# The query product of a window attention block, from quarters of TensorE's array to halves

## The chip, the cores and the metric

The kernel runs on one core of a Trainium2 chip. The metric is the device time of one execution in microseconds (us); lower is better. Five engines matter here: PE is TensorE (matrix products), PEld the loads of its stationary operand, which run beside it, DVE is VectorE, ACT is ScalarE, POOL is GpSimd. SP issues most DMAs.

## The reference

The input x has 32 sequences of 512 tokens with 256 features. One transformer block is computed in float32. In `[...]` are shapes.

```python
x = x + attn(layernorm(x))       # x [32, 512, 256]
x = x + ffn(layernorm(x))

# attn: 16 heads of 64, 4 key/value heads, causal window of 128
q = rmsnorm((x @ wq.T).reshape(B, T, 16, 64), q_norm_w)   # the query product: 256 -> 1024
k = rmsnorm((x @ wk.T).reshape(B, T, 4, 64), k_norm_w)
v = (x @ wv.T).reshape(B, T, 4, 64)
scores = where(0 <= i - j < 128, q . k / 8, -inf)
y = softmax(scores) @ v
return y @ wo.T

# ffn: a product of 256 x 256, and 8 gated low-rank pairs of rank 16
gate = softmax(x @ gate_w.T)
return x @ weight.T + (gate-weighted sum of V_e (U_e x)) / 16
```

The change touches only how the query product `x @ wq.T` is put on TensorE.

## The kernel before

**Tiles.** The work is cut into 128 tiles of 128 tokens (4 for each sequence). A tile passes through a pipeline of some 17 steps: layer norm statistics, the turned input xT (features on partitions, `trx`), the key/value product `kv_pe` (line 447), the query product (`qa_pe` and `qb_pe`, lines 486 and 491), norms of q and k, the scores in four parts `s_pe(3)` to `s_pe(0)` (line 606), softmax, the weighted values `y_pe` and `yb_pe` (lines 722 and 739), the output product `o_pe` (line 757), and the second half with `ug_pe`, `base_pe` and `lora_pe` (lines 813, 816, 863; the product's own line is 808 for the first two, 864 for the third).

**Order.** Nothing is scheduled by the compiler. The order on every engine is the order in which the program calls these steps. For the tiles in the middle that order is in `slot(i)` (line 894), called for i from 17 to 127; the pipeline is filled by a list of steps by hand, FIRST, and drained by another, LAST. On TensorE a slot calls, each for another tile:

`s_pe(0)`, `kv_pe`, `ug_pe`, `base_pe`, `o_pe`, `lora_pe`, `s_pe(3)`, `y_pe`, `s_pe(2)`, `qa_pe`, `yb_pe`, `s_pe(1)`, `qb_pe`, and then `s_pe(0)` of the next slot.

In each slot the steps `kv_pe` to `lora_pe` use the whole array of 128 rows by 128 columns, and everything from `s_pe(3)` to the next `s_pe(0)` uses quarters of 64 rows by 64 columns. So the array changes from quarters to the whole and back once in a slot. Over the whole program the order holds 157 changes from quarters to the whole and 157 back.

**The query product.** Its result for a tile is 128 tokens by 1024 columns and fills two PSUM banks, `q0` and `q1`, of 512 columns each; the 256 input features come in two chunks `c` of 128 partitions. The first six tiles use `q_pe` (line 463) on the whole array. The other 122 use `q_product` (line 473), called twice. `qa_pe` is the pass with r = 0: the upper 64 partitions of each chunk go to bank `q0`, the lower 64 to bank `q1`. `qb_pe` is the pass with r = 1, with the banks swapped, and so completes both sums. In a pass, for each chunk, each half m of the 128 tokens (64 columns of the stationary operand xT, written to 64 partitions of the bank) and each bank, there is one matmul that streams 512 columns of `wq_sb`. That is 8 matmuls of the program. Each float32 matmul of the program appears as two pairs of a weight load and a matmul in the profile, so a pass has 16 records, and the 122 tiles have 122 x 2 x 16 = 3904.

After `qa_pe`, ACT reads one column of bank `q1` (`q_mark`, line 499). After `qb_pe`, ACT reads both banks twice: `q_copy` (line 502, records at line 505) and `qsq` (line 507, records at line 510).

Of the kernel before, what the change touches and what calls it, by code (L numbers as in the profile page):

```python
# [19 lines left out]
ND = D // P  # L20
# [11 lines left out]
def tile_window_attn_lora_ffn(  # L32
# [45 lines left out]
    nc = tc.nc  # L78
# [8 lines left out]
    H = P // 2  # L87
# [194 lines left out]
    wq_sb = const.tile([P, ND, QD], F32, name="wq_sb")  # L282
# [11 lines left out]
    for c in range(NB):  # L294
        rows = slice(c * BL, (c + 1) * BL)
# [12 lines left out]
    for e, cmp in enumerate((ALU.is_ge, ALU.is_gt)):  # L308
        rows = slice(e * H, (e + 1) * H)
# [106 lines left out]
    class Tile:  # L416
# [55 lines left out]

        def q_product(self, r, start, stop):
            for c in range(ND):
                for m in range(2):
                    for gp in (r, 1 - r):
                        rows = slice((gp ^ r) * H, (gp ^ r) * H + H)
                        nc.tensor.matmul(  # L478
                            self.ps[f"q{gp}"][m * H : (m + 1) * H, :],
                            self.xT[rows, c, m * H : (m + 1) * H],  # L480
                            wq_sb[rows, c, gp * 512 : (gp + 1) * 512],
                            start=(start and c == 0), stop=(stop and c == ND - 1),
                            skip_group_check=True,
                        )

        def qa_pe(self):
            for gp in range(GP):
# [694 lines left out]
```

## Time and profile before

| what | value |
|---|---|
| median of 3 runs | 1947.53 us (1945.81 to 1948.91) |
| profiled execution, its own time | 1946.66 us |
| its span, first to last instruction | 1944.9 us |
| granted TensorE clock, mean | 1.000 |
| matmuls of the query product, line 478 | 3904, mean 590 ns, 64 x 64 of the array, 512 columns |
| its weight loads | 3904, mean 133 ns, 64 columns |
| matmuls of kv, line 450 | 512, mean 618 ns, 128 x 128 of the array, 512 columns |
| its weight loads | 512, mean 189 ns, 128 columns |
| PE busy from 300 to 1700 us | 1400.0 of 1400 us |

How to read it: the profile's lines give the program's line, the engine, the operation, output and inputs, the part of the array (rows\*columns), the shape, a count, the busy time and the mean duration. Matmuls are pipelined: the duration of one runs from its start to its modelled end and overlaps the next, so the time that a stage holds TensorE is read from the starts of stages, or from the chain of work that ended last, in which each piece is counted once.

### The profile page before, as it was taken

How to read it: one execution, taken by the hardware profiler on the slowest of the kernel's cores; microseconds unless marked ns; L12 is line 12 of the kernel's file. 1: busy time of each engine (PE TensorE's matmuls, PEld its weight loads, DVE VectorE, ACT ScalarE, POOL GpSimd, SP SyncE). 2: the span in 40 equal slices, each digit the busy share in tenths (PEclk: the TensorE clock that was granted, in tenths of full speed). 3: DMA queues.
4: the chain of work that ended last, by engine and by line, in shares of the span. 5: the costliest groups of instructions: out<-in, count | busy, mean ns of one | idle time of the engine just before them, and what ended most of it. 6: DMA issues, size and time to landing. Idle time of an engine off the chain costs nothing.

```text
span 1944.9 us, 61511 instructions
## 1 busy us (share of the span) xinstructions
PE 1931.6 (99%) x21677; PEld 1332.0 (68%) x21677; DVE 1714.8 (88%) x4958; ACT 1523.6 (78%) x6407; POOL 1628.1 (84%) x1103
## 2 busy tenths in 40 slices
PE   8999999999999999999999999999999999999999
PEld 4566676676677666766766777667667666776677
DVE  6999889998989988899889899888998898998894
ACT  6888777877888787778878777887787787877783
POOL 6998889888898888898888988888988889888872
PEclk9999999999999999999999999999999999999999
DMA  5676767767676676776676767776776767667663
GB/s 128 140 157 156 157 154 158 156 154 159 156 158 155 155 160 155 156 160 153 155 158 155 160 154 158 158 157 152 157 159 154 159 154 161 152 153 161 145 145 93
DMA packets 273060, 297.90 MB, mean 153 GB/s; under 512 B 172272, under 2 KB 206704, under 8 KB 272752
## 3 DMA queue, kind: packets, MB, share of 16 engines
q1 hardware_dynamic: 272208, 292.40, 67.3%
q8 instruction: 172, 2.82, 0.7%
q10 hardware_dynamic: 544, 1.57, 0.2%
q14 instruction: 136, 1.11, 0.2%
HBM read 36.71 MB, written 16.78 MB: 28 GB/s over the span
## 4 chain that ended last, share of the span: by engine, by line
PE 91%; SPq 5%; ACT 1%; DVE 1%; DMA 1%; issue 1%; POOL 1%; ACTq 0%; DVEq 0%; POOLq 0%
PE o_ps L760 21%; PE q_ps L478 20%; PE y_ps L709 15%; PE s_ps_S L620 12%; PE kv_ps L450 11%; PE f_ps L808 5%; SPq L401 4%; PE g_ps L808 3%; PE f_ps L864 3%; ACT ex L648 1%; DMA pT<-tr 1%; SPq L269 1%; PE q_ps L466 1%; DVE tr L414 0%; POOL other L688 0%
## 5 line engine op out<-in xcount | busy, mean ns | idle before, releaser
L648 ACT ACTIVATE ex<-s_ps_S,nmax 128x128 f32<-128x128 f32 x2048 | 719.6, 373 | 17.3 <-DVE nmax L637 10.4
L660 POOL TENSOR_TENSOR ex<-ex,rden 128x1024 f32<-128x1024 f32 x256 | 485.3, 1896 | 238.4 <-DVE rden L656 238.3
L478 PE MATMUL q_ps<-wq_sb,xT 64*64 64x512 f32 x3904 | 470.8, 590 | 0.1
L760 PE MATMUL o_ps<-wo_sb,yT 128*128 128x256 f32 x2048 | 463.7, 379 | 0.3 <-ACT yT L751 0.2
L364 POOL TENSOR_TENSOR rs<-ss_eps,minus_half 128x20 f32<-128x20 f32 x128 | 453.5, 3543 | 3.3 <-ACT ss_eps L525 3.3
L648 ACT ACTIVATION_READ_ACCUMULATOR ex<-s_ps_S,nmax 128x1 f32 x2048 | 435.6, 213 | 0.0
L760 PEld LDWEIGHTS o_ps<-wo_sb,yT 128*128 128x128 f32 x2048 | 388.3, 190 | 56.8 <-issue 2.0
L414 DVE STREAM_TRANSPOSE tr<-ex 128x256 f32<-128x256 f32 (+1 forms) x1280 | 399.3, 358 | 2.9 <-POOL ex L660 1.1
L620 PEld LDWEIGHTS s_ps_S<-kT,pT 64*64 64x64 f32 x8000 | 264.5, 133 | 131.4 <-issue 50.8
L637 DVE TENSOR_REDUCE nmax<-s_ps_S 128x4 f32<-128x512 f32 x512 | 343.6, 672 | 1.2
L620 PE MATMUL s_ps_S<-kT,pT 64*64 64x144 f32 (+8 forms) x8000 | 324.1, 273 | 2.1 <-ACT kT L598 1.1
L709 PE MATMUL y_ps<-pT,kv 64*64 64x256 f32 x4096 | 272.8, 377 | 0.6 <-ACT kT L598 0.6
L688 POOL TENSOR_TENSOR other<-pT,mixed 128x512 f32<-128x512 f32 x192 | 241.1, 1276 | 32.0 <-DMA pT<-tr 21.3
L450 PE MATMUL kv_ps<-wkv_sb,xT 128*128 128x512 f32 x512 | 253.4, 618 | 0.6 <-DVE xT L442 0.2
L478 PEld LDWEIGHTS q_ps<-wq_sb,xT 64*64 64x64 f32 x3904 | 157.4, 133 | 126.1 <-issue 123.6
L542 POOL TENSOR_TENSOR q<-q,rs 128x1024 f32<-128x1024 f32 x128 | 243.1, 1899 | 0.0
L709 PEld LDWEIGHTS y_ps<-pT,kv 64*64 64x64 f32 x4096 | 165.7, 133 | 88.9 <-issue 60.4
L510 ACT ACTIVATE qsq<-q_ps,ln_rs_a 128x512 f32<-128x512 f32 x256 | 177.3, 695 | 45.6 <-PE q_ps L478 42.3
L632 DVE COPY_PREDICATED s_ps_S<-over,s_ps_S 128x128 f32<-128x128 int32 x512 | 146.0, 286 | 50.2 <-PE s_ps_S L620 42.0
L497 ACT COPY mark_y<-y_ps 128x1 f32<-128x1 f32 x128 | 20.6, 161 | 207.5 <-PE y_ps L709 207.4
L505 ACT ACTIVATE q<-q_ps,ln_rs_a 128x512 f32<-128x512 f32 x256 | 163.2, 689 | 0.2 <-PE q_ps L478 0.2
L414 DVE STREAM_TRANSPOSE tr<-q 128x1024 f32<-128x1024 f32 x125 | 154.3, 1234 | 2.7 <-POOL q L542 2.7
(95 smaller groups left out, 2601.9 us busy)
## 6 DMA issues: line engine op xcount, KB each, us to landing
pT<-tr SPq DMA_DIRECT2D x1888, 116.0 KB, 2.3
x<-in_x_dram SPq DMA_DIRECT2D x128, 128.0 KB, 2.6
xb<-in_x_dram SPq DMA_DIRECT2D x256, 64.0 KB, 2.4
out_dram<-res SPq DMA_DIRECT2D x128, 128.0 KB, 2.0
pT<-tr SPq DMA_DIRECT2D x64, 104.0 KB, 2.2
pT<-tr SPq DMA_DIRECT2D x48, 112.0 KB, 2.3
pT<-tr SPq DMA_DIRECT2D x48, 76.0 KB, 2.1
wq_sb<-in_wq_dram ACTq DMA_DIRECT2D x1, 1024.0 KB, 7.1
```

What stands on the lines that cost most here:

```text
L364: nc.gpsimd.tensor_tensor(o, v, minus_half[:, : o.shape[-1]], ALU.pow)
L414: after_moves(nc.vector.transpose(out, in_), n - 2)
L450: nc.tensor.matmul(ps, self.xT[:, c, :], wkv_sb[:, c, :], start=(c == 0), stop=(c == ND - 1))
L478: nc.tensor.matmul(self.ps[f"q{gp}"][m * H : (m + 1) * H, :], self.xT[rows, c, m * H : (m + 1) * H], wq_sb[rows, c, gp * 512 : (gp + 1) * ...
L542: nc.gpsimd.tensor_tensor(self.q_n.rearrange("p (g d) -> p g d", d=HD), self.q.rearrange("p g (h d) -> p (g h) d", d=HD), self.rs[:, :NH]. ...
L620: mm = nc.tensor.matmul(ps[m * H : (m + 1) * H, half, gp, lo:hi], qT[rows, c0 : c0 + H], self.s.kT[rows, gp, k0 + lo : k0 + hi], start=Tru ...
L637: nc.vector.tensor_reduce(self.nmax[j], ps[:, :, :, :P], AX.X, ALU.max, negate=True)
L648: nc.scalar.activation(self.ex[e][:, c, gp, half], ps[:, gp, half, :P], AF.Exp, bias=self.nmax[j][:, gp, half : half + 1], accum_out=self. ...
L660: nc.gpsimd.tensor_tensor(ex, ex, self.rden[e].rearrange("p c g a -> p (c g a)").unsqueeze(2).to_broadcast([P, 8, P]), ALU.mult,)
L688: mul = nc.gpsimd.tensor_tensor(self.other[:, hh].rearrange("p y (n k) -> p y n k", k=BL), self.probs(0)[:, hh].rearrange("p y (n k) -> p ...
L709: mm = nc.tensor.matmul(ps[:, gp], v[:, v0 : v0 + HD], w[:, :, w0 : w0 + H].rearrange("p (m y) k -> p m y k", m=2), start=start, stop=stop ...
L760: nc.tensor.matmul(ps[:, :D], self.yT[:, c].rearrange("p e t -> p (e t)"), wo_sb[:, c, :], start=(c == 0), stop=(c == NCH - 1),)
```

## The change

`q_product` loses its loop over the two halves of the tokens. A matmul now takes all 128 tokens of a chunk as its stationary operand and writes all 128 partitions of a bank; its 64 rows, the 512 streamed columns, the order of chunks and banks, and the accumulation are as before. A pass has 4 matmuls of the program (8 records in the profile) on halves of 64 rows by 128 columns. Nothing else is changed: the order of steps, the banks, the other products.

```diff
         def q_product(self, r, start, stop):
             for c in range(ND):
-                for m in range(2):
-                    for gp in (r, 1 - r):
-                        rows = slice((gp ^ r) * H, (gp ^ r) * H + H)
-                        nc.tensor.matmul(
-                            self.ps[f"q{gp}"][m * H : (m + 1) * H, :],
-                            self.xT[rows, c, m * H : (m + 1) * H],
-                            wq_sb[rows, c, gp * 512 : (gp + 1) * 512],
-                            start=(start and c == 0), stop=(stop and c == ND - 1),
-                            skip_group_check=True,
-                        )
+                for gp in (r, 1 - r):
+                    rows = slice((gp ^ r) * H, (gp ^ r) * H + H)
+                    nc.tensor.matmul(
+                        self.ps[f"q{gp}"], self.xT[rows, c, :],
+                        wq_sb[rows, c, gp * 512 : (gp + 1) * 512],
+                        start=(start and c == 0), stop=(stop and c == ND - 1),
+                        skip_group_check=True,
+                    )
```

## The prediction

> **What bounds the kernel now.** I read the profiled execution: its span is 1944.9 us and its own time 1946.66 us, so 1.8 us lie around the span. All sums below are made against 1946.66; the median of the three runs, 1947.53, is 0.9 us (0.04%) above it. First the head of the page, for the engines and TensorE's clock:
>
> ```profile
> PE 1931.6 (99%) x21677; PEld 1332.0 (68%) x21677; DVE 1714.8 (88%) x4958; ACT 1523.6 (78%) x6407; POOL 1628.1 (84%) x1103
> PEclk9999999999999999999999999999999999999999
> PE 91%; SPq 5%; ACT 1%; DVE 1%; DMA 1%; issue 1%; POOL 1%; ACTq 0%; DVEq 0%; POOLq 0%
> L478 PE MATMUL q_ps<-wq_sb,xT 64*64 64x512 f32 x3904 | 470.8, 590 | 0.1
> ```
>
> TensorE is busy for 99% of the span, holds 91% of the chain that ended last, and its clock is full in every slice. A busy PE need not be a bound one, so I asked next who waits for whom. All PE waits but the first load's 5.4 us come to 4.3 us (1.3, 1.1, 0.6, 0.4, 0.3, 0.2, 0.2, 0.2); the longest that ended in an s_ps_S matmul are
>
> ```profile
> PE s_ps_S L620 <- ACT ex L648: 1.3, 4, 0.6
> PE s_ps_S L620 <- ACT kT L598: 1.1, 3, 0.6
> ```
>
> So nothing holds TensorE up; what TensorE needs for a tile is what a tile costs: 1944.9 / 128 = 15.2 us. Any time added to TensorE's stream reaches the end nearly whole. The other engines work in fixed orders; a later TensorE can make none of TensorE's inputs later by more than the delay itself, so the added time is also the most that the end can move.
>
> The third view is the timeline of PE alone, one line for each stage (start, length, engine, line, operation, array part, count). The lengths overlap, because matmuls are pipelined; the starts are what counts.
>
> ```profile
> 1003.16 0.59 PE L864 MATMUL f_ps<-wv_sb,uT 128*128 128x256 f32 x2
> 1003.69 0.72 PE L620 MATMUL s_ps_S<-kT,pT 64*64 64x144 f32 x16
> 1004.23 1.04 PE L709 MATMUL y_ps<-pT,kv 64*64 64x256 f32 x16
> 1005.09 0.67 PE L620 MATMUL s_ps_S<-kT,pT 64*64 64x144 f32 x16
> 1005.58 1.90 PE L478 MATMUL q_ps<-wq_sb,xT 64*64 64x512 f32 x16
> 1007.30 1.04 PE L709 MATMUL y_ps<-pT,kv 64*64 64x256 f32 x16
> 1008.16 0.67 PE L620 MATMUL s_ps_S<-kT,pT 64*64 64x144 f32 x16
> 1008.65 1.90 PE L478 MATMUL q_ps<-wq_sb,xT 64*64 64x512 f32 x16
> 1010.37 0.67 PE L620 MATMUL s_ps_S<-kT,pT 64*64 64x144 f32 x16
> 1010.97 1.98 PE L450 MATMUL kv_ps<-wkv_sb,xT 128*128 128x512 f32 x4
> 1012.79 0.63 PE L808 MATMUL g_ps<-wf_sb,hT 128*128 128x136 f32 x4
> ```
>
> The reader is to see three things. (a) A q pass lasts 1007.30 - 1005.58 = 1.72 us: sixteen records of 512 columns in four steps of 0.43 us, four quarters at work beside each other. (b) Between stages on quarters there is no gap: s takes 0.49 us from start to start (1008.16 to 1008.65), as often as it stands before another stage on quarters. (c) Where the array goes from quarters to the whole or back, time is lost. The last s stage, at 1010.37, should hand over at 1010.86; kv starts at 1010.97, 0.11 later. Its four records of 0.43 should then end at 1012.69; g starts at 1012.79, another 0.10. Going back, f starts at 1003.16 with two steps of 0.215, so s is due at 1003.59 and starts at 1003.69, 0.10 late; y is due 0.49 later, at 1004.18, and starts at 1004.23, another 0.05. By starts, then, a change to 128-column loads costs 0.21 us and one back to 64-column loads 0.15. The chain that ended last, read over a steady stretch, gives the same two prices from stage to stage:
>
> ```profile
> 914.41 1.73 PE y_ps L709 x32
> 916.14 0.49 PE s_ps_S L620 x16
> 916.63 1.72 PE q_ps L478 x16
> 918.34 0.86 PE y_ps L709 x16
> ...
> 921.90 1.91 PE kv_ps L450 x4
> ...
> 929.03 0.65 PE s_ps_S L620 x16
> ```
>
> kv takes 1.91 instead of 1.72, so 0.19 for entering; the s stage after f takes 0.65 instead of 0.49, so 0.16 for leaving. Together 0.35 (0.36 by starts).
>
> **The change, part by part.** *Fewer, wider matmuls.* Each pass drops from 16 records on quarters to 8 on halves, 64 rows by 128 columns. Two row halves can stand beside each other instead of four quarters, so there are again 8 / 2 = 4 steps of 512 columns. A step takes 0.43 us on four quarters (0.43 x 4 = 1.72) and on the whole array (kv, 1.72 without its entry), so I take it as 0.43 on halves: **gain 0**. The halves themselves are not in the trace. Its bounds: below, the four records of a step start some 0.007 us apart (single records of the trace), and two fewer could give back 0.013 us a pass, 244 x 0.013 = 3 us in all; above, halves that don't run beside each other take 8 steps, 244 x 4 x 0.43 = +420 us. I take 0, since one tile (kv) and four (q) keep the same step.
>
> The Trainium skill, page "TensorE: Matmul & The Clock Gate", section "Measured speedup vs the span model", puts about 4 ns on every further tile of a packed group; two fewer in four steps would be 32 ns a pass and an estimated 8 us saved. The rows above speak against it: a step of four tiles is as long as a step of one.
>
> *Weight loads.* 64-column loads take 133 ns, 128-column loads 190 ns by their groups. Both are issued under the step before and are covered by its 430 ns; even two loads of 190 in a row are 380. Cost **0** inside a pass. Without that cover a load stands open; that is the second part (0.10 and 0.05) of the switch prices above.
>
> *Switches of the array's division.* This is the term that decides. In the written order of PE, 239 of the 244 passes (122 tiles, two passes each) come after an s or y stage on quarters, and 238 are followed by one: qa stands between s and yb, qb between s and the next s. Today those 477 seams cost nothing. After the change each is a change between quarters and halves, with rows as before and columns from 64 to 128. The other 11 seams of q stand next to a stage on the whole array; they are changes of division already and stay so. The trace has no seam where only the columns change, so this price is bounded: at least 0 (the seams s to q and q to s today), at most the whole change's 0.21. The nearest row is the change between quarters and the whole array, of which all 314 that the order holds are of this kind. I take its price from the chain, since these are the terms that add up to the span: 239 x 0.19 + 238 x 0.16 = 45.4 + 38.1 = **83.5 us**. By starts it is 239 x 0.21 + 238 x 0.15 = 85.9.
>
> The Trainium skill, page "TensorEngine Tiling (Array Packing)", section "Key Properties", says that changing the tiling mode, and not merely the tile, drains TensorE, and lists 64x64 and 64x128 as different modes. By it the full price is due; by the row of today's seams it would be nothing. No row here shows a seam between those two modes.
>
> *What else moves.* Nothing is moved in any engine's order, no wait or DMA is added. ACT's mark_q and its two readers of the q banks get their data about 0.35 us later; ACT is at 78%, and it waits 43.6 and 42.3 us for these today. DVE (88%) and POOL (84%) have room, which grows with the span. Of the 4.3 us that TensorE waits, some will be swallowed by the slower stream: between 0 and -4; I take 0.
>
> **Sum:** 1946.66 + 83.5 = **2030 us**, +4.3%.
>
> **The rivals.**
> - *Part of the price only.* The stop for the last step to run out (0.10 a switch) stays but the load is hidden, 477 x 0.10 = 48, 1994 us; or the load is open (0.10 and 0.05) but nothing is stopped, 239 x 0.10 + 238 x 0.05 = 36, 1982 us. For it: the rows' division doesn't change. Against it: both parts always come together in the trace.
> - *The seam is free.* If the stop hangs on the division of the rows, a quarter-to-half seam is like s to q today, 0.00 us, and the kernel stays at 1947, not slower. For it: every row half keeps its own rows through the seam, and today each loads its next weights under the running step. Against it: in the trace every change of load width costs, without exception. It decides if the price of a seam is under 4 / 477 = 0.008 us.
> - *Loads one after the other.* If the two 128-column loads that stand open after a switch follow each other, an entry costs 0.19 more: 2030 + 239 x 0.19 = 2075.
> - *No halves beside each other*: 2030 + 420 = 2450; the four quarters that run today by both rows and columns speak against it.
> - *Faster by the shorter steps alone*: 1944 if seams are free; more than that nothing in the profile offers, as TensorE's steps have the same 512 columns.
>
> **How the numbers follow.** Full price 71%: 2013 (477 x 0.14, the cheaper way for all) to 2047 (477 x 0.21). Part of it 9%, free 12%, loads in a row 4%, no halves together 2%, faster 2%. Full and partial price make 80%, so the range is 1981 to 2047. This kernel's measurement can tell about 0.2% (4 us) from no change: faster by more than that 2%, within it 12%, slower 86%.
>
> **What would show it.** In the changed profile: L478 has 1952 records, 64 rows by 128 columns, with 512 columns; q pieces of the chain go from 1.72 to about 1.91 and the s and yb pieces after them from 0.49 and 0.86 to about 0.65 and 1.02; s before q, kv, g, f, o stay; the clock stays full; DVE and POOL fall to 84 and 80%. If q stays 1.72 and the next stage starts without delay, the free seam is right; if q becomes 3.4, the halves don't run together. I am wrong above all if a seam between quarters and halves has no price.

## The result, and the profile after

The changed kernel takes 2031.19 us (median of 4 runs, 2029.48 to 2032.97) against 1947.43 us for the kernel before in the same comparison: a ratio of 1.0428, 95% interval 1.0416 to 1.0441. That is 83.8 us more; the forecast was 2030 us, 83.5 more. The profiled execution has a span of 2029.3 us, 84.4 more than before. Two executions of the later comparisons, one of the kernel before at 5188 us and one of the strips at 2501 us, stand far outside their groups and are left out of every ratio below.

The head of the page after, with the lines that answer to those of before (two source lines are gone, so line 478 is now 477, and later lines are two lower):

```profile
PE 2016.8 (99%) x19725; PEld 1316.2 (65%) x19725; DVE 1738.8 (86%) x4958; ACT 1524.4 (75%) x6407; POOL 1628.8 (80%) x1103
PEclk9999999999999999999999999999999999999999
PE 97%; SPq 2%; DMA 1%; ACT 1%; issue 0%; DVE 0%; ACTq 0%; DVEq 0%
L477 PE MATMUL q_ps<-wq_sb,xT 64*128 64x512 f32 x1952 | 485.5, 615 | 0.1
```

TensorE still holds the end, now with 97% of the chain, at a full clock, although it runs 1952 matmuls fewer: half of the 3904 of line 478. The others gain idle share, as they must when the span grows. TensorE's waits are as small as before, 3.8 us in all without the first load, against 4.3 (two of the lines of the list of waits):

```profile
PE y_ps L707 <- ACT kT L596: 1.8, 1, 1.8
PE s_ps_S L618 <- ACT ex L646: 0.4, 1, 0.4
```

So the added time is not a wait for another engine; it lies inside TensorE's own stream. The timeline of PE shows where (start, length, engine, line, operation, part of the array; the lengths overlap, read the starts):

```profile
1016.43 0.67 PE L618 MATMUL s_ps_S<-kT,pT 64*64 64x144 f32 x16
1017.03 1.99 PE L477 MATMUL q_ps<-wq_sb,xT 64*128 64x512 f32 x8
1018.94 1.09 PE L707 MATMUL y_ps<-pT,kv 64*64 64x256 f32 x16
1019.86 0.42 PE L618 MATMUL s_ps_S<-kT,pT 64*64 64x144 f32 x7
```

s is through at 1016.43 + 0.49 = 1016.92; q starts at 1017.03, 0.11 later. Its four steps of 0.43 should end at 1018.75; y starts at 1018.94, 0.19 later: about 0.10 because the first step of q stood behind its open load, and about 0.10 for the way back. y should hand over 0.86 later, at 1019.80; s starts at 1019.86, 0.06 later, for y's own open load. Together that is 0.36 us. The chain that ended last gives the sums:

```profile
970.25 0.49 PE s_ps_S L618 x16
970.74 1.92 PE q_ps L477 x8
972.65 1.02 PE y_ps L707 x16
973.68 0.49 PE s_ps_S L618 x16
974.17 1.92 PE q_ps L477 x8
976.09 0.65 PE s_ps_S L618 x16
```

q has gone from 1.72 to 1.92, the yb after it from 0.86 to 1.02, the s after the second pass from 0.49 to 0.65; the s stages in front of q are unchanged. That is 0.36 for a pass. Laid beside each other by the start of the same tile's kv product, the two traces part by 0.72 us with every tile of the slots, evenly from the first slot to the last.

### The profile page after: what moved, and what is told of

Read it like the earlier page. It is cut to its first block, busy times and chain, and to the rows that moved or that the text cites. A ratio compares the mean times of both kernels' runs of the same rounds, so it can differ in the third digit from the quotient of the medians.

```text
span 2029.3 us, 57489 instructions
## 1 busy us (share of the span) xinstructions
PE 2016.8 (99%) x19725; PEld 1316.2 (65%) x19725; DVE 1738.8 (86%) x4958; ACT 1524.4 (75%) x6407; POOL 1628.8 (80%) x1103
## 4 chain that ended last, share of the span: by engine, by line
PE 97%; SPq 2%; DMA 1%; ACT 1%; issue 0%; DVE 0%; ACTq 0%; DVEq 0%
PE q_ps L477 23%; PE o_ps L758 21%; PE y_ps L707 16%; PE s_ps_S L618 13%; PE kv_ps L450 12%; PE f_ps L806 5%; PE g_ps L806 3%; PE f_ps L862 3%; SPq L401 1%; PE q_ps L466 1%; DMA pT<-tr 0%; ACT ex L646 0%; DMA wkv_sb<-in_wkv_dram 0%; PE ckv_ps_mean L347 0%; PE cqa_ps_mean L347 0%
## 5 line engine op out<-in xcount | busy, mean ns | idle before, releaser
L477 PE MATMUL q_ps<-wq_sb,xT 64*128 64x512 f32 x1952 | 485.5, 615 | 0.1
L646 ACT ACTIVATION_READ_ACCUMULATOR ex<-s_ps_S,nmax 128x1 f32 x2048 | 450.9, 221 | 0.0
L618 PEld LDWEIGHTS s_ps_S<-kT,pT 64*64 64x64 f32 x8000 | 241.5, 133 | 163.0 <-ACT yT L749 86.4
L618 PE MATMUL s_ps_S<-kT,pT 64*64 64x144 f32 (+7 forms) x8000 | 323.1, 276 | 0.5 <-ACT kT L596 0.4
L477 PEld LDWEIGHTS q_ps<-wq_sb,xT 64*128 64x128 f32 x1952 | 169.0, 186 | 159.1 <-issue 145.7
L707 PEld LDWEIGHTS y_ps<-pT,kv 64*64 64x64 f32 x4096 | 144.0, 132 | 124.5 <-ACT ln_v_a L376 84.9
L749 ACT COPY yT<-y_ps 128x512 f32<-128x512 f32 x256 | 150.5, 609 | 7.4 <-PE y_ps L707 7.4
```

Of the source, the lines that this page charges most:

```text
L477: nc.tensor.matmul(self.ps[f"q{gp}"], self.xT[rows, c, :], wq_sb[rows, c, gp * 512 : (gp + 1) * 512], start=(start and c == 0), stop=(stop ...
L618: mm = nc.tensor.matmul(ps[m * H : (m + 1) * H, half, gp, lo:hi], qT[rows, c0 : c0 + H], self.s.kT[rows, gp, k0 + lo : k0 + hi], start=Tru ...
L646: nc.scalar.activation(self.ex[e][:, c, gp, half], ps[:, gp, half, :P], AF.Exp, bias=self.nmax[j][:, gp, half : half + 1], accum_out=self. ...
L707: mm = nc.tensor.matmul(ps[:, gp], v[:, v0 : v0 + HD], w[:, :, w0 : w0 + H].rearrange("p (m y) k -> p m y k", m=2), start=start, stop=stop ...
```

## The experiments

**The theory:** every change of the array's division between two stages costs TensorE about 0.10 us of standstill and the open load of the next stage's first weights, 0.10 for 128 columns and 0.05 for 64; 477 new seams of this kind are the whole loss. **The rivals:** wide matmuls or wide loads cost something by themselves; halves are a special, slow case; the price hangs on one side of the division (rows or columns) only.

**One pass of the two on halves.**

```diff
-                for m in range(2):
+                for m in range(1 if r == 0 else 2):
...
+                        cols = slice(0, P) if r == 0 else slice(m * H, (m + 1) * H)
```

> Only the first pass of each tile (qa) stands on halves, the second (qb) on quarters as before. Price at the seams (0.19 in, 0.16 out): 122 passes are left with a price, so half of the 83.8 us, about 1947 + 42 = 1989 us, and in the chain the first q piece of a slot is 1.91 and the second 1.72. A cost that comes only once per tile with the first wide pass: 2031. A cost of the reordered bank use between the two passes (the second pass waiting for the mark): 1947.

Measured: 1990.3 us, ratio 1.0222 (1.0205 to 1.0239), 43 us more than before, half of the loss. The chain has both kinds of pass next to each other:

```profile
952.65 1.92 PE q_ps L479 x8
954.57 1.02 PE y_ps L710 x16
955.59 0.49 PE s_ps_S L621 x16
956.08 1.72 PE q_ps L479 x16
957.80 0.49 PE s_ps_S L621 x16
```

The pass on halves costs 1.92 and makes its successor 1.02; the pass on quarters costs 1.72, and its successor the usual 0.49. The loss is paid by each pass for itself.

**One chunk of the two on halves.** As above with `c == 0` in place of `r == 0`, in both passes.

> In both passes the first chunk of features (c = 0) stands on halves and the second on quarters: half of the wide matmuls, but as many seams, since each pass still has one entry and one way back. Price at the seams: unchanged, about 2031 us (0.19 before the first chunk, 0.16 in the middle of the pass instead of after it). Price of the wide matmuls or wide loads themselves: half, about 1989 us.

Measured: 2031.6 us, ratio 1.0431 (1.0416 to 1.0447), as slow as the full change with half of its wide matmuls. Of this kernel's chain:

```profile
955.05 2.08 PE q_ps L479 x12
957.13 0.86 PE y_ps L710 x16
```

q now holds both prices itself (1.72 + 0.36 = 2.08), since the way back to quarters lies in its middle, and the y after it is back at 0.86. The number of seams sets the loss, not the number of wide matmuls or loads. The rival of a price by the matmul is out.

**The whole array in the same places.** Instead of halves, the first pass computes bank q0 and the second q1 on 128 rows by 128 columns.

```diff
-            self.q_product(0, True, False)
+            self.q_pe(0)
...
-            self.q_product(1, False, True)
+            self.q_pe(1)
```

> The passes stay where they are in the order, but each computes one bank on the whole array (128 rows by 128 columns), the first q0, the second q1; the mark after the first reads q0. Any change of the array's division has the same price: about 2031 us (within 4), as with halves. If halves are special (a step of two halves or their loads cost something that a whole-array matmul does not): clearly under 2031, down to 1947.

Measured: 2027.95 us, ratio 1.0412 (1.0397 to 1.0428). Its q pieces take 1.91, the y after them 1.02, the s after the second pass 0.65:

```profile
953.43 1.91 PE q_ps L466 x4
955.35 1.02 PE y_ps L707 x16
```

Halves are no special case: an excursion to the whole array costs the same to within 4 us. (What makes the 3 to 4 us between the two is known in part only: by the starts of kv, a tile falls back by 0.716 us here and by 0.723 with halves, which is under 1 us in all.)

**Halves beside the whole array**, to see a seam at which only the rows change: qb is moved behind the next `s_pe(0)`, directly in front of `kv_pe`. The same move with qb on quarters is its control.

```diff
         at(i - 6).s_pe(0)
...
+        if i > 17:
+            at(i - 3).qb_pe()
         at(i - 3).kv_pe()
...
-        at(i - 3).q_copy(1)
         at(i - 3).q_copy(0)
+        at(i - 3).q_copy(1)
...
-        at(i - 2).qb_pe()
```

> The changed kernel, but qb stands behind the next slot's s_pe(0), directly before kv_pe (111 of the 122 tiles), and ACT copies q0 before q1. For each such tile the way out of qb (0.16) and the entry of kv (0.19) go, and one seam from halves to the whole array comes, at which only the rows change. If a change of rows alone has the full price of a 128-column entry (0.19 to 0.21): 2031 - 111 x 0.15 = about 2014 us. If it is free: 2031 - 111 x 0.35 = about 1992 us.

> Control for the moved qb: the kernel before, with qb on quarters behind the next slot's s_pe(0), directly before kv_pe, and ACT copying q0 before q1. No seam is added or taken away, so 1947 us within 4. If the move itself costs by waits on the q banks, it shows here as idle time of PE before base_pe or o_pe, and what it costs is to be taken off the run with halves beside kv.

Measured: 2063.34 us with halves (ratio 1.0595, 1.0579 to 1.0610) and 2022.97 us with quarters (1.0390, 1.0376 to 1.0404). Both expectations missed on the time, because the move itself costs 76 us, and it does so in a place I had not named. The control's list of waits:

```profile
PE s_ps_S L620 <- ACT ex L648: 51.1, 114, 0.8
```

Before, this wait was 1.3 us in all. `s_pe(0)` now follows `s_pe(1)` at once, and it writes a bank that ACT's eight exponentials of part 2 must have read. The 1.72 us of qb between the two had covered them. With halves the same wait is smaller:

```profile
PE s_ps_S L618 <- ACT ex L646: 24.1, 107, 0.8
```

That fits the way back from halves: the exponentials follow ACT's mark on q, which waits for the end of qa, and the yb behind qa takes 1.02 us instead of 0.86, as in the changed kernel, so that ACT gets more time. (The list counts only what lies outside the modelled matmuls; by starts, the score stages are 77 and 49 us late, with nearly the same difference.) The two runs can still be set against each other. Halves should add 111 x (0.35 + 0.19) + 11 x 0.70 = 67.6 us to the control (qa both ways and the way into qb for the moved tiles; both passes for the other 11), less the 51.1 - 24.1 = 27.0 us of waits: 40.6. Measured: 40.4. In that sum the seam from halves to the whole array costs what the seam from quarters costs, and the chain of the run with halves shows it directly:

```profile
908.87 1.92 PE q_ps L477 x8
910.79 1.91 PE kv_ps L450 x4
```

kv takes 1.91, not 1.72, behind a stage that has as many columns as kv itself. A change of rows alone has the full price too.

**Both banks on the whole array, in front of kv.** The two passes and the mark are gone from the slot; `q_pe(0)` and `q_pe(1)` stand behind `s_pe(0)`.

> For 111 tiles both banks of the query product are computed on the whole array directly before kv_pe, inside the stretch that is on the whole array anyway; no mark. As many wide records as with halves (8 + 8 a tile), but no added seam. Price at the seams: 1947 us, within 5. Price of wide matmuls or wide loads: about 2024 us. Fewer instructions worth something by themselves: below 1942.

Measured: 2218.49 us, ratio 1.1394 (1.1377 to 1.1412): a miss by 270 us, most of it for the same reason as the control, now that neither pass stands between the score stages. Its list of waits begins

```profile
PE s_ps_S L620 <- ACT ex L648: 199.9, 224, 1.7
```

So its time says nothing on the price of wide matmuls. Its chain does:

```profile
901.18 3.63 PE q_ps L466 x8
904.81 1.72 PE kv_ps L450 x4
```

The eight records on the whole array take 8 x 0.43 us and one entry of 0.19, and kv, which stands right behind them on the same division, takes 1.72 with no price. Wide matmuls and loads cost nothing where the division doesn't change. The run also says that the two passes, where they stand in the order, cover the softmax, and that this move to the whole-array stretch gives the cover up.

**Column halves for the other products.** q stays on quarters; kv, g, f, o and the low-rank product use two halves of 128 rows by 64 columns beside each other.

```diff
-                    ps, self.xT[:, c, :], wkv_sb[:, c, :], start=(c == 0), stop=(c == ND - 1)
+                for m in range(2):
+                    t = slice(m * H, (m + 1) * H)
...
+                        ps[t], self.xT[:, c, t], wkv_sb[:, c, :],
```

> The kernel before, with q on quarters, and kv, g, f, o and the low-rank product on halves of the other kind, 128 rows by 64 columns, two beside each other; so at the 157 entries and 157 ways back only the rows change, and the load that stands open at an entry has 64 columns. If a change of rows alone costs as much as any: entry 0.11 + 0.05 instead of 0.11 + 0.10, so 157 x 0.05 = 8 us less, about 1939 us. If a change of rows alone is free: 1947 - 157 x 0.35 = about 1892 us. If column halves do not run beside each other: over 2800 us.

Measured: 1947.41 us, ratio 1.0006 (0.9996 to 1.0015): no gain. But the chain shows the shorter open load:

```profile
920.26 0.49 PE s_ps_S L623 x16
920.75 1.87 PE kv_ps L452 x8
```

kv is 1.87 instead of 1.91, and by the starts of kv the two traces part by 0.047 us with each tile of the slots. At the last tile this kernel is 4.3 us ahead of before; at the end of the span it is 0.4 ahead. It loses the rest after the last kv, where the list that drains the pipeline mixes these products with transposes on the whole array, so that new seams arise: the traces have 49 changes of division behind the last kv here, and 30 before, so 3.9 us for 19 more of them. Rows-only seams are not free; the standstill of 0.10 is there.

**Column halves, and column strips of 32, in the slots only.** The lists that fill and drain stay on the whole array.

```diff
+        parts["of"] = 2
         for i in range(17, N - 1 + 1):
             slot(i)
+        parts["of"] = 1
```

> As with column halves (128 rows by 64 columns) for kv, g, f, o and the low-rank product, but only in the 111 slots; in the lists that fill and drain the pipeline these products stay on the whole array, as their transposes do. A change of rows alone has the full stop, and only the open load of an entry is shorter: 111 x 0.05 = 5.2 us less, about 1942 us (0.26% under before). If the loss that swallowed the gain of the earlier run came from something other than the seams to the transposes in the drain: no change, 1947.

> The same with four strips of 128 rows by 32 columns side by side. If the open load at an entry lasts in proportion to its columns (0.105 for 128, 0.05 for 64), 32 columns leave 0.026: 111 x 0.078 = 8.7 us less than before, about 1938 us. If the load has a floor near that of 64 columns, or if four strips make the steps longer (the shortest, of 136 columns, last 0.116 us): 1942 or more.

Measured: with halves 1944.89 us against 1948.37 in the same comparison, ratio 0.9983 (0.9974 to 0.9992). This version is faster than the kernel before by 3.5 us (0.17%); 5.2 were expected. By the starts of kv a slot gains the 0.047 us that were due, but now and then the trace falls back, and the score matmuls wait 3.2 us for ACT's exponentials instead of 1.3. With strips 1949.32 us, ratio 1.0002 (0.9993 to 1.0011): no gain, although the open load at the entry is down to 0.025 us (the start of kv's second step behind its first), as expected. A slot gets 0.06 us shorter as long as nothing disturbs it, 111 x 0.06 = 6.7 us in all, but every few tiles the trace falls back, by up to 0.8 us at a time and by 6.7 us in all. In the lists of waits the score matmuls wait 6.9 us (17 times) for ACT's exponentials, against 1.3 us (4 times) before; and ACT's copy of kT waits 104 us for DMAs, against 47 before and 69 with halves. At each of the three largest setbacks there is one wait of kT of 2.4 to 2.6 us and one of a score matmul of 0.6 to 0.7. The page's chain shows that other things than TensorE hold more of the end:

```profile
PE 68%; SPq 16%; DMA 4%; ACT 4%; DVE 3%; POOL 3%; issue 2%; ACTq 0%; DVEq 0%; POOLq 0%
```

TensorE had 91% before, and SP's queue 5%; with halves in the slots it is 82 and 8.

**The three loads of x on ACT's queue**, to see whether SP's queue swallows the gain: with column halves, with the kernel before as a control, and with strips.

```diff
-                nc.sync.dma_start(xb[b][k * BL : (k + 1) * BL, :, c], src[k, c])
+                feed().dma_start(xb[b][k * BL : (k + 1) * BL, :, c], src[k, c])
...
+        return nc.scalar if feeder["slots"] else nc.sync
```

> Column halves in the slots as before, and the three loads of x of a slot are issued by ACT's queue instead of SP's, behind the slot's last copy. If SP's queue is what is late next (its share of the chain that ended last grew from 5% to 8% with halves and 16% with strips), SP's share falls back and the gain of 5.2 us comes whole: about 1942 us. If the issues cost ACT what they save SP (three of about 0.5 us on an engine that TensorE's scores wait for): 1945 or more.

> Control: the kernel before with the three loads of x of a slot on ACT's queue. TensorE's stream is untouched and hardly waits, so if ACT can issue them in its idle time: 1947 us within 3. If ACT's issues delay the exponentials: over 1950.

> The four strips in the slots with the three loads of x on ACT's queue. If SP's queue swallowed the strips' gain: 1947 - 111 x 0.06 = about 1940 us (the open load is 0.078 shorter, the four staggered records of a step give back 0.02). If something else did: 1947 to 1950 as with the strips alone.

Measured, as ratios to the kernel before: halves 1.0069 (1.0056 to 1.0081), the control 1.0079 (1.0065 to 1.0093), strips 1.0100 (1.0084 to 1.0115). All are slower, the control by 15 us, so the move costs more than what it was to show; and SP's share of the chain doesn't fall (13, 10 and 18%). That SP's queue is next in line is not shown by this. By the traces, the strips' gain goes into waits for ACT, and ACT's copy of kT waits longer for DMAs (in the control of this move too, 107 us instead of 47); why these come later stays open.

## Why the prediction was right, point by point

- *TensorE bounds the kernel, and added time arrives whole.* Right. 0.36 us a pass, by starts, is 239 x 0.21 + 238 x 0.15 = 85.9 us; 84.4 arrived in the span. Some of the difference is the start, with TensorE's first matmul at 5.1 us instead of 5.4, and its other waits, 3.8 us instead of 4.3. The forecast counted 239 entries and 238 ways back; the changed trace has 238 and 239, which moves the sum by less than 0.1 us.
- *Fewer and wider matmuls gain nothing, halves keep the step.* Right: a step is 0.43 us with two halves too (weight loads of one pass at 971.20 and 971.63 in the trace), and the run with one chunk on halves, where half of them are wide, is no slower or faster than the full change.
- *Loads inside a pass are covered.* Right; only the first load behind a seam stands open.
- *A seam at which only the columns change has the full price.* Right. This was the only term with a wide bound, 0 to 0.21, and I had no row for it, only the nearest one. The price read from the chain, 0.19 and 0.16, came out as 0.20 and 0.16. The lower end of the range, 2013, was priced with 0.14 a seam; no row has that, and the cheaper row of 0.15 gives 2018.
- *The sum.* 83.5 forecast from the chain's rows, 83.8 measured between medians. The two digits of those rows leave an uncertainty of 477 x 0.005 = 2.4 us, and by starts the same seams come to 85.9, so that the agreement to 0.3 us is luck.
- *The rivals.* A free seam would have left 1947; a part of the price 1982 to 1994; loads one after the other 2075: in the trace two 128-column loads behind a seam run together (0.19 us for the pair, at 970.67). All three are out by more than 35 us. Halves that don't run beside each other (2450) are out by the step of 0.43 us, and a faster kernel (1944) by the sign.
- *What would show it.* The records, the pieces of q, yb and s, the clock and POOL's 80% came as listed. DVE fell to 86%, not 84: its busy time rose by 24 us, of which I had said nothing.

The Trainium skill, page "TensorEngine Tiling (Array Packing)", section "Key Properties", has the rule that a change of tiling mode drains TensorE. The runs agree in so far as TensorE stands still for about 0.10 us at every change of division, where only the columns change (quarters to row halves) and where only the rows do (row halves to the whole, quarters to column halves).

The Trainium skill, page "TensorE: Matmul & The Clock Gate", section "LDWEIGHTS (loading the stationary operand)", makes a load's time its columns divided by 1.2, in ns, whatever its rows. An estimate by it is 107, 53 and 27 ns for 128, 64 and 32 columns. The open loads measured here agree: 105, 51 and 25 ns (the first step behind the seam is that much longer: in this change, with column halves and with column strips). The loads' own records are longer, 186 ns for 128 columns and 133 for 64.

## What to carry to other kernels

Before a product is put on another part of TensorE's array, look at its neighbours in the order: where they stand on a different division, each seam cost the standstill and the next stage's open load here (0.36 us for an excursion there and back), with eight records in the excursion or with four. Count the seams, price them from a seam of any kind that the trace already shows, and check in the waits that nothing hides them. And a stage that looks free to move between two others may be the cover of a slower engine: here 1.72 us of the query product stood between two score stages and hid eight exponentials.

## What the runs showed of the hardware that was not expected

- The price of a seam does not depend on which side of the array's division changes: behind the stream of the last matmul 0.09 to 0.10 us pass in every kind that was run (quarters to row halves, to column halves, to column strips, to the whole; row halves to the whole).
- Two column halves of 128 rows run beside each other as the two row halves do, in steps of 0.43 us for 512 columns; four strips of 32 columns too (1.85 us for kv).
- DVE's differences of v (128 x 256, `vdiff`) took 508 ns on average after the change against 392 before, 11 us in all, with the same shapes and count; ACT's exponentials took 381 against 373. With one pass or one chunk on halves the first is 508 and 500 too, in the control with quarters 396. The cause is open. Neither engine held the end.
